# Two reorderings in a cross-attention kernel: where four probability casts stand while the pipeline fills, and the order of work as it drains

## The chip, the cores and the metric

The kernel runs on one core of a Trainium2 chip. The metric is the device time in microseconds (us), lower is better. A core has five engines, each with its own instruction stream that runs strictly in its written order: TensorE (PE, matrix products; its weight loads are shown as PEld), VectorE (DVE), ScalarE (ACT), GpSimd (POOL) and SyncE (SP), which here does nothing but issue DMA transfers. They meet through semaphores.

## What is computed

Cross-attention with four separate key sets per batch element. With 32 batch elements, 512 query rows, 640 channels, 20 heads of 32 channels, the inputs give 77 context rows, so that the first key set ("text", 77 keys) takes all of them and the other three are empty:

```python
q = _heads(hidden_states @ to_q_w)
h_txt = _sdpa(q, _heads(ehs_txt @ to_k_w), _heads(ehs_txt @ to_v_w))
...
out = _merge(h_txt) + ...
out = out @ to_out_w + to_out_b
out = (out + residual) / RESCALE
```

`_sdpa` is `softmax(q k^T / sqrt(32)) v` for each head, and the residual is the input itself.

## The kernel before

All products are made in pairs of numbers: every float32 operand is split into a high part (a cast to TensorE's rounded float32 type, made by ACT) and a low part (the operand less its high part, made by DVE or POOL), and a product is the sum of three matmuls: high by high, high by low, low by high.

**Opening (lines 294 to 383).** Keys and values of all batch elements are computed and put into DRAM scratch. Then comes the main pipeline.

**Groups and slots.** The 20 heads of a batch element are taken four at a time: five groups per element, `N` = 160 in all. Group `n` is batch element `b = n // 5` and chunk `j = n % 5`. `slot(n)` (line 661) writes out the instructions of all engines for one step of the pipeline, and the order in which it does so is the order of each engine's queue; no scheduler reorders anything. In slot `n`:

- PE: `scores(n, t)` for the four blocks `t` of 128 queries (three matmuls each; VectorE then reduces each block to the negated row maxima `nm`, line 462, and that reduction is queued right behind), `queries(n + 1)` in two parts of 6 and 9 matmuls, `values(n - 3)` (6 matmuls, line 546), and the output product of an earlier batch element, cut into pieces.
- ACT: `exps(n, t)`, four exponentials for each block (line 472); the high part of the next queries (`split_q`, line 103); the high parts of the probabilities of group n - 3 (`cast_p`, line 518, and the first line of `rest_p`, line 524); the copy `aw` that the sum of the attention's halves begins with (`sum_a`, line 557); the high part of the attention result of group n - 4 (`high_a`, line 566).
- DVE: the reductions; the low part of most of the probabilities (`rest_p`, line 525); the reciprocals of the row sums of group n - 1 (`sums`, line 482); low parts of the attention result (`low_a`, line 571) and of the queries (line 104); the transposition of the probabilities of group n - 1 into the single buffer `z` (`transpose_p`, line 494); the two additions of `sum_a` (line 559); the emptying of finished output banks (`finish`, line 618).
- POOL: `last_p` (line 532), the last low part of the probabilities; `normalize(n - 1)` (line 487), which multiplies the exponentials by the reciprocals and which the transposition waits for; low parts of the input `xt` (line 264); `add_bias` (line 582).
- SP: `load_p(n - 2)` (lines 510, 511) reads transposed probabilities from DRAM scratch `pd` into `raw`; then keys or values of the coming groups (`refill`), inputs `xs`, residual rows `xr`; the four transfers of `transpose_p` (line 501) that write `z` to `pd`; output rows.

So the probabilities of group n travel: normalized and transposed in slot n + 1, written to `pd`, loaded into `raw` in slot n + 2, cast and multiplied by the values in slot n + 3. Buffers that matter: `z` one, `raw` two, the parts `pp` one, the attention's bank pair `pa` one, banks for scores `sc` three, for queries `pq` one, and for the output `po` two. A third output bank can be begun only when VectorE has emptied the first.

**Two orders of the casts.** In a slot with output work (`has_out`; every slot from 7 on) `cast_p` opens the slot on ACT, ahead of the exponentials. The slots that have a group to take but no output product yet, 3, 4, 5 and 6, are marked `filling` (line 672); there the three functions stand behind the exponentials of the second block (line 711).

**The end.** The last slot, 159, returns after `values(156)` and the additions of `sum_a(156)`. `end()` (line 771) then writes out what is left: the last transposition, the attention's parts of group 156, the probabilities of 157, pieces 6 to 9 of the output of batch element 30, and then, with `take(157)`, `take(158)`, `take(159)` between them, the output of the last element. `piece(last - 1, 6)` closes the bank of rows block 2, first half, and then uses the other bank; `piece(last - 1, 7)` closes that one and begins block 3 in the bank that was closed first. `finish()` empties all banks that are closed.

Of the kernel before, what the change touches and what calls it, by code (L numbers as in the profile page):

```python
# [51 lines left out]
def kernel(  # L52
# [34 lines left out]
    N = B * NC_  # L87
# [403 lines left out]
    def transpose_p(n):  # L491

        pn = pnb[n % 2]
        nc.vector.transpose(  # L494
            z.rearrange("p b t j -> p t b j"),
            pn.rearrange("p (t h) k -> p t (h k)", t=NQ).rearrange("p t (b i) -> p t b i", i=Q),
        )
        pd = dram.tile([(NBLK + 2) * Q, S], F32, tag="pd", name="pd", bufs=6)
        rows = pd[: NBLK * Q].rearrange("(b i) q -> i b q", i=Q)
        for a in range(4):  # L500
            nc.sync.dma_start(
                rows[:, :, a * P : (a + 1) * P],
                z[a * Q : (a + 1) * Q].rearrange("p b t j -> p b (t j)"),
            )
        pds[n] = pd
# [8 lines left out]
    def cast_p(n):  # L514

        raw = raws[n]
        pp = late[0].tile([P, 5, S], FPR, tag="pp", name="pp", bufs=1)
        nc.scalar.copy(pp[:, 0:2, :], raw[:, 0:2, :])  # L518
        pps[n] = pp

    def rest_p(n):

        raw, pp = raws[n], pps[n]
        nc.scalar.copy(pp[:64, 4, :], raw[:64, 2, :])  # L524
        nc.vector.tensor_tensor(  # L525
            pp[:, 2:4, :], raw[:, 0:2, :], pp[:, 0:2, :].bitcast(F32), ALU.subtract
        )

    def last_p(n):

        raw, pp = raws.pop(n), pps[n]
        nc.gpsimd.tensor_tensor(  # L532
            pp[64:, 4, :], raw[:64, 2, :], pp[:64, 4, :].bitcast(F32), ALU.subtract
        )
# [26 lines left out]
    def high_a(n):  # L561
        if n >= N - NC_ + 1:
            at = xpool[0].tile([P, 2, S], FPR, tag="xt", name="at", bufs=7)
        else:
            at = late[0].tile([P, 2, S], FPR, tag="at", name="at", bufs=8)
        nc.scalar.copy(at[:, 0, :], pas[n][:, 0])
        ats[n] = at
# [93 lines left out]
    def slot(n, beside=()):  # L661
        b, j = divmod(n, NC_)
        ahead, more = n + 1 < N, b + 1 < B
        back, first = PIECES[j]
        bo_, has_out = b - back, b >= back
        xsplits = SPLIT_X.get(j, ((), ())) if more and n > LATE else ((), ())
        turns = TRANSPOSE_X.get(j, ((), (), ())) if more and b else ((), (), ())
        if b == 1 and j < 2:
            turns = (((), (), ()), ((0, 1), (2,), ()))[j]
        taken = takes.get(n)  # L670

        filling = taken is not None and not has_out
        if not filling:
            refill(b, j, 0)
        if taken is not None and not filling:
            cast_p(taken)
        if n - 1 in takes:
            high_a(takes[n - 1])
        s = scores(n, 0)
        if taken is not None and not filling:  # L680
            rest_p(taken)
        rs = sums(n - 1) if n else None
        if taken is not None and not filling:
            last_p(taken)
        if n:
            normalize(n - 1, rs)
        if n - 1 in takes:
            low_a(takes[n - 1])
        exps(n, 0, *s)
        if ahead:  # L690
            queries(n + 1, 0, 2)
        s = scores(n, 1)
        if n - LAG + 1 in pds and n > LATE:
            load_p(n - LAG + 1)
        if filling:
            refill(b, j, 0)
        if n == NC_:
            load_x(b + 1, (2, 3))
        for k in WO.get(n, ()):
            nc.sync.dma_start(wos[0][:, k].bitcast(F32), wo_dram[:, k].bitcast(F32))  # L700
        refill(b, j, 1)
        finish()
        if j == 4 and b and b + 2 < B:
            load_x(b + 2, (0, 1))
        if j in RESIDUAL and b >= RESIDUAL[j][0]:
            load_residual(b - RESIDUAL[j][0], RESIDUAL[j][1])
        if j in BIAS and b >= BIAS[j][0]:
            add_bias(b - BIAS[j][0], BIAS[j][1])
        exps(n, 1, *s)
        if filling:  # L710
            cast_p(taken)
            rest_p(taken)
            last_p(taken)
        for i in turns[0]:
            transpose_x(b + 1, i)
        if ahead:
            queries(n + 1, 2, NC_)
        s = scores(n, 2)
        if not ahead:
            exps(n, 2, *s)  # L720
            piece(bo_, first)
            s = scores(n, 3)
        if j == 3 and has_out:
            piece(bo_, first)
            finish()
        if n and has_out:
            transpose_p(n - 1)
        if ahead:
            split_q(n + 1)
            exps(n, 2, *s)  # L730
        if n and not has_out:
            transpose_p(n - 1)
        if j == 4 and b + 2 < B:
            load_x(b + 2, (0, 1) if not b else (2, 3))
        for c in xsplits[0]:
            split_x(b + 1, c)
        if not ahead:
            exps(n, 3, *s)
            normalize(n, sums(n))
            finish()  # L740
            piece(bo_, first + 1)
            values(taken)
            sum_a(taken)
            return
        if has_out:
            if j != 3:
                piece(bo_, first)
        else:
            s = scores(n, 3)
        if taken is not None:  # L750
            values(taken)
        if len(beside) > 0:
            context_values(LAST, beside[0], psv)
        if has_out:
            s = scores(n, 3)
        finish()
        for i in turns[1]:
            transpose_x(b + 1, i)
        if taken is not None:
            sum_a(taken)  # L760
        for c in xsplits[1]:
            split_x(b + 1, c)
        exps(n, 3, *s)
        if len(beside) > 1:
            context_values(LAST, beside[1], psv)
        if has_out:
            piece(bo_, first + 1)
        for i in turns[2]:
            transpose_x(b + 1, i)

    def end():


        last = B - 1
        load_p(N - 2)
        transpose_p(N - 1)
        high_a(N - 4)
        low_a(N - 4)
        cast_p(N - 3)
        rest_p(N - 3)  # L780
        last_p(N - 3)
        add_bias(last - 1, 3)
        piece(last - 1, 6)
        finish()
        piece(last - 1, 7)
        finish()
        load_p(N - 1)
        load_residual(last, 0)
        load_residual(last, 1)
        piece(last - 1, 8)  # L790
        take(N - 3)
        piece(last - 1, 9)
        cast_p(N - 2)
        rest_p(N - 2)
        last_p(N - 2)
        finish()
        spare = late[0].tile([P, 3, S], F32, tag="raw", name="xr", bufs=2)
        load_residual(last, 3, spare.rearrange("p k q -> p (k q)")[:, :C])
        load_residual(last, 2)

        def begin(i, j0, j1):
            t, h = divmod(i, 2)
            if j0 == 0:
                if i < 3:
                    pos[last, t, h] = ps.tile([P, S], F32, tag="sc", name="po", bufs=3)
                elif i == 3:
                    pos[last, t, h] = ps.tile([P, S], F32, tag="pq", name="po", bufs=1)
                elif i < 6:
                    output_bank(last, t, h)
                else:  # L810
                    if i == 6:
                        pas[N] = late[1].tile([P, 2, S], F32, tag="pa", name="po", bufs=1)
                    pos[last, t, h] = pas[N][:, i - 6]
            for j in range(j0, j1):
                project(last, t, h, j)

        begin(0, 0, 2)
        begin(1, 0, 2)
        take(N - 2)
        cast_p(N - 1)  # L820
        rest_p(N - 1)
        last_p(N - 1)
        for t in (0, 1, 3, 2):
            add_bias(last, t)
        begin(2, 0, 3)
        begin(0, 2, 4)
        begin(1, 2, 4)
        begin(2, 3, 4)
        begin(3, 0, 4)
        take(N - 1)  # L830
        begin(4, 0, 4)
        begin(5, 0, 4)

        def close(t):
            for h in range(2):
                project(last, t, h, 4)
                closed.append((last, t, h))
            finish()

        close(0)  # L840
        close(1)
        begin(6, 0, 4)
        close(2)
        begin(7, 0, 4)
        close(3)
# [65 lines left out]
```

## Time and profile before

Three timed runs lie between 1954.48 and 1955.75 us, with a median of 1954.53. The profiled execution took 1951.98 us; its span, from the first to the last instruction, is 1949.9 us. All positions below are us from the start of that span.

| stretch | us | PE busy | DVE busy | ACT busy | POOL busy | granted PE clock | DMA share |
|---|---|---|---|---|---|---|---|
| 0 to 301.87: keys, values, slots 0 to 2 | 301.87 | 290.97 | 134.82 | 93.80 | 53.67 | 0.99 | 0.84 |
| 301.87 to 344.74: slots 3 to 6 | 42.87 | 33.28 | 28.15 | 34.80 | 21.41 | 0.89 | 0.84 |
| 344.74 to 1895: slots 7 to 158 | 1550.26 | 1540.34 | 1249.10 | 1386.52 | 920.25 | 1.00 | 0.86 |
| 1895 to 1949.9: last slot and end | 54.90 | 40.70 | 25.57 | 18.79 | 19.84 | 0.94 | 0.48 |

A row gives the time in which each engine was at work within the stretch. "Granted PE clock" is the share of its full clock that the throttle let TensorE have. On PE's queue, slot 3 begins at 301.87 (first matmul of `scores`), slot 4 at 313.61, slot 5 at 324.56, slot 6 at 334.38 and slot 7 at 344.74.

In a timeline line the columns are start, duration, engine, line of the kernel, operation, what it writes and reads, how many; in brackets, how long the engine stood idle before it and who released it. In a line of the chain of waits the columns are start, duration and what the chain passed through.

### The profile page before, as it was taken

To read this page: it belongs to the slowest core of one execution; us is meant where nothing else is said; L and a number is where in the kernel's file an instruction comes from. 1 tells how busy PE (TensorE), PEld (TensorE's weight loads), DVE (VectorE), ACT (ScalarE), POOL (GpSimd) and SP (SyncE) were. 2 spreads that over 40 slices of the span, in tenths; PEclk is the share of its full clock that TensorE was granted. 3 is DMA by queue.
4 is the path that set the end of the run, shared out by engine and by line. 5 is a ranking of instruction groups with operands and counts; after the bars stand their busy time and mean duration, and the time that the engine had idled before them with its cause. 6 is when DMAs were issued, how large, how long until landed. Compare 5 with 4: busy or idle time off the path is not lost.

```text
span 1949.9 us, 36251 instructions
## 1 busy us (share of the span) xinstructions
PE 1905.3 (98%) x10332; PEld 1701.3 (87%) x10332; DVE 1437.6 (74%) x2334; ACT 1533.9 (79%) x6210; POOL 1015.2 (52%) x668
## 2 busy tenths in 40 slices
PE   9999998999999999999999999999999999999997
PEld 7787896889889989988889989988989999888896
DVE  4444345887888788787888878788888888877874
ACT  3232237898988898888888888898989989888982
POOL 1100055566556655555556555566655665556543
PEclk9999999999999999999999999999999999999999
DMA  9878878888888888988888888888889888888874
GB/s 185 190 188 232 201 198 215 222 226 230 228 225 230 227 229 228 239 232 218 227 238 233 229 225 228 236 232 224 228 232 237 227 229 225 225 224 232 230 201 144
DMA packets 560919, 431.28 MB, mean 221 GB/s; under 512 B 187024, under 2 KB 469072, under 8 KB 560720
## 3 DMA queue, kind: packets, MB, share of 16 engines
q1 hardware_dynamic: 556208, 414.46, 82.3%
q0 software_dynamic: 4416, 14.34, 2.2%
q8 instruction: 84, 1.38, 0.3%
q14 instruction: 115, 0.94, 0.2%
q10 hardware_dynamic: 96, 0.16, 0.0%
HBM read 247.17 MB, written 181.64 MB: 220 GB/s over the span
## 4 chain that ended last, share of the span: by engine, by line
PE 20%; ACT 19%; issue 17%; DMA 15%; DVE 13%; POOL 12%; SPq 2%; DVEq 0%; POOLq 0%; ACTq 0%
ACT pn L472 10%; POOL pn L487 8%; DMA raw<-pd 7%; DMA pd<-z 6%; PE pq L435 5%; PE po L589 5%; POOL pp L532 4%; DVE pp L525 3%; ACT xt L263 3%; ACT aw L557 3%; PE pk L191 2%; PE pv L191 2%; PE sc L454 2%; DVE nm L462 2%; DVE z L494 2%
## 5 line engine op out<-in xcount | busy, mean ns | idle before, releaser
L472 ACT ACTIVATE pn<-sc,nm 128x77 f32<-128x77 f32 x2560 | 802.5, 335 | 70.9 <-DVE nm L462 68.0
L589 PE MATMUL po<-wo_s,at 128*128 128x320 f32 x3840 | 624.3, 310 | 17.7 <-DVE xr L618 14.4
L435 PE MATMUL pq<-xt,wq_s 128*128 128x512 f32 x2400 | 605.4, 393 | 0.0
L589 PEld LDWEIGHTS po<-wo_s,at 128*128 128x128 f32 x3840 | 575.4, 188 | 27.8 <-DVE xr L618 24.6
L532 POOL TENSOR_TENSOR pp<-raw,pp 64x512 fp32r<-64x512 f32 x160 | 211.8, 1324 | 643.6 <-ACT pp L524 413.4
L472 ACT ACTIVATION_READ_ACCUMULATOR pn<-sc,nm 128x1 f32 x2560 | 545.1, 213 | 0.0
L435 PEld LDWEIGHTS pq<-xt,wq_s 128*128 128x128 f32 x2400 | 436.8, 188 | 75.1
L454 PE MATMUL sc<-kb,qt 128*128 128x308 f32 x1920 | 377.5, 305 | 1.3 <-ACT pn L472 0.5
L487 POOL TENSOR_TENSOR pn<-pn,rs 128x1232 f32<-128x1232 f32 x160 | 364.4, 2277 | 24.7 <-DVE rs L482 12.6
L494 DVE STREAM_TRANSPOSE z<-pn 128x1280 f32<-128x1280 f32 x160 | 241.8, 1511 | 168.8 <-POOL pn L487 158.4
L454 PEld LDWEIGHTS sc<-kb,qt 128*128 128x128 f32 x1920 | 325.7, 189 | 45.0 <-ACT pn L472 1.6
L462 DVE TENSOR_REDUCE nm<-sc 128x4 f32<-128x308 f32 x640 | 295.1, 462 | 46.4 <-PE sc L454 44.1
L546 PE MATMUL pa<-pp,vb 128*128 128x512 f32 x960 | 256.0, 401 | 10.5 <-ACT pp L518 4.8
L525 DVE TENSOR_TENSOR pp<-raw,pp 128x1024 fp32r<-128x1024 f32 x160 | 195.6, 1222 | 88.2 <-ACT pp L518 78.9
L559 DVE TENSOR_TENSOR pa<-pa,aw 64x512 f32<-64x512 f32 x320 | 222.6, 696 | 34.7 <-ACT aw L557 25.2
L557 ACT COPY aw<-pa 64x1024 f32<-64x1024 f32 x160 | 162.0, 1012 | 79.6 <-PE pa L546 77.4
L264 POOL TENSOR_TENSOR xt<-xs,xt 128x512 fp32r<-128x512 f32 x160 | 204.3, 1296 | 37.1 <-ACT xt L263 35.3
L546 PEld LDWEIGHTS pa<-pp,vb 128*128 128x128 f32 x960 | 175.3, 190 | 43.8 <-ACT pp L518 5.8
L582 POOL TENSOR_TENSOR xr<-xr,bias 128x640 f32<-128x640 f32 x128 | 201.5, 1575 | 0.2
L518 ACT CAST pp<-raw 128x1024 fp32r<-128x1024 f32 x160 | 168.9, 1055 | 33.0 <-DMA raw<-pd 33.0
L191 PE MATMUL pk<-ct,wk_s 128*128 128x512 f32 (+1 forms) x600 | 137.9, 388 | 9.1 <-ACT ct L103 6.4
L191 PEld LDWEIGHTS pk<-ct,wk_s 128*128 128x128 f32 x600 | 114.2, 191 | 31.1 <-ACT ct L103 7.3
(43 smaller groups left out, 1358.0 us busy)
## 6 DMA issues: line engine op xcount, KB each, us to landing
pd<-z SPq DMA_DIRECT2D x640, 160.0 KB, 3.8
raw<-pd SPq DMA_DIRECT2D x160, 512.0 KB, 4.0
xs<-in_x_dram SPq DMA_DIRECT2D x128, 320.0 KB, 6.2
xr<-in_x_dram SPq DMA_DIRECT2D x128, 320.0 KB, 4.1
out_dram<-xr SPq DMA_DIRECT2D x127, 320.0 KB, 4.1
raw<-pd SPq DMA_DIRECT2D x160, 128.0 KB, 4.2
v_dram<-vs SPq DMA_DIRECT2D x80, 192.0 KB, 3.9
k_dram<-ks POOLq DMA_DIRECT2D x20, 512.0 KB, 3.7
```

What stands on the lines that cost most here:

```text
L191: nc.tensor.matmul(held[j][:, :gn], w[:, k, a, :], cts[g, k][:, c, :gn], start=(k == 0 and n == 0), stop=(k == NK - 1 and n == 2),)
L435: nc.tensor.matmul(pqs[n], wq_s[:, k, a, j * P : (j + 1) * P], xts[b, k][:, c, :], start=(k == 0 and m == 0), stop=(k == NC_ - 1 and m == 2),)
L454: nc.tensor.matmul(sc[:, :KCOLS], qt[:, a, t * P : (t + 1) * P], kb[:, j - GROUPS[g][0], c], start=(m == 0), stop=(m == 2),)
L462: nc.vector.tensor_reduce(nm, sc[:, :KCOLS].rearrange("p (h k) -> p h k", k=NKEY), AX.X, ALU.max, negate=True)
L472: nc.scalar.activation(pnb[n % 2][:, at, :NKEY], sc[:, i * NKEY : (i + 1) * NKEY], AF.Exp, bias=nm[:, i : i + 1], accum_out=sms[n][:, at : ...
L487: nc.gpsimd.tensor_tensor(pf, pf, rs.unsqueeze(2).to_broadcast([P, NQ * HPC, NKEY]), ALU.mult)
L494: nc.vector.transpose(z.rearrange("p b t j -> p t b j"), pn.rearrange("p (t h) k -> p t (h k)", t=NQ).rearrange("p t (b i) -> p t b i", i=Q),)
L525: nc.vector.tensor_tensor(pp[:, 2:4, :], raw[:, 0:2, :], pp[:, 0:2, :].bitcast(F32), ALU.subtract)
L532: nc.gpsimd.tensor_tensor(pp[64:, 4, :], raw[:64, 2, :], pp[:64, 4, :].bitcast(F32), ALU.subtract)
L546: nc.tensor.matmul(pas[n][:, p, :], vb[:, p, t, :], pp[:, c, :], start=(c == p), stop=(t == 1),)
L559: nc.vector.tensor_tensor(pa[64 * p : 64 * p + 64, 0], pa[:64, p], aw[:, p], ALU.add)
L589: nc.tensor.matmul(pos[b, t, h][:, :HALF], ats[b * NC_ + j][:, a, t * P : (t + 1) * P], wos[0][:, j, c, h * HALF : (h + 1) * HALF], start= ...
```

## The change

In `slot`, the condition `not filling` is taken off `cast_p`, `rest_p` and `last_p`, and the separate place for filling slots is removed: slots 3 to 6 take the order that all later slots have. `refill` keeps its two places. In `end`, piece 6 and the emptying of its closed bank come first; the casts of group 157 on ACT keep their order after `high_a`; `low_a` stands behind `cast_p`, which are on different engines; and the last transposition, with its four transfers, comes behind the second `finish`.

```diff
@@ slot
         filling = taken is not None and not has_out
         if not filling:
             refill(b, j, 0)
-        if taken is not None and not filling:
+        if taken is not None:
             cast_p(taken)
         if n - 1 in takes:
             high_a(takes[n - 1])
         s = scores(n, 0)
-        if taken is not None and not filling:
+        if taken is not None:
             rest_p(taken)
         rs = sums(n - 1) if n else None
-        if taken is not None and not filling:
+        if taken is not None:
             last_p(taken)
...
         exps(n, 1, *s)
-        if filling:
-            cast_p(taken)
-            rest_p(taken)
-            last_p(taken)
         for i in turns[0]:
             transpose_x(b + 1, i)
@@ end
         load_p(N - 2)
-        transpose_p(N - 1)
+        piece(last - 1, 6)
+        finish()
         high_a(N - 4)
+        cast_p(N - 3)
         low_a(N - 4)
-        cast_p(N - 3)
         rest_p(N - 3)
         last_p(N - 3)
         add_bias(last - 1, 3)
-        piece(last - 1, 6)
-        finish()
         piece(last - 1, 7)
         finish()
+        transpose_p(N - 1)
         load_p(N - 1)
```

## The prediction

> **What bounds it now.** I read the busy shares first, then the waits of TensorE, then busy time by stretch, then the timelines of the two places that the change touches.
>
> ```profile
> PE 1905.3 (98%) x10332; PEld 1701.3 (87%) x10332; DVE 1437.6 (74%) x2334; ACT 1533.9 (79%) x6210; POOL 1015.2 (52%) x668
> ```
>
> TensorE bounds the middle: between 345 and 1895 it waits 8.1 us in all. A lead won ahead of that stretch is carried through it; the end is a chain of its own. The end first, a timeline from 1904:
>
> ```profile
> 1904.40 1.43 DVE L559 TENSOR_TENSOR pa<-pa,aw 64x512 f32<-64x512 f32 x2 [0.57 <-ACT aw L557]
> 1905.86 0.59 ACT L566 CAST at<-pa 128x512 fp32r<-128x512 f32 x1 [1.49 <-DVE pa L559]
> 1906.35 1.05 ACT L518 CAST pp<-raw 128x1024 fp32r<-128x1024 f32 x1
> ...
> 1908.64 1.51 DVE L494 STREAM_TRANSPOSE z<-pn 128x1280 f32<-128x1280 f32 x1 [2.81 <-DMA pd<-z]
> ...
> 1910.07 0.65 DVE L571 TENSOR_TENSOR at<-pa,at 128x512 fp32r<-128x512 f32 x1
> ...
> 1910.65 1.34 DVE L525 TENSOR_TENSOR pp<-raw,pp 128x1024 fp32r<-128x1024 f32 x1
> 1911.91 0.87 DVE L618 TENSOR_TENSOR xr<-po,xr 128x320 f32<-128x320 f32 x2
> 1912.44 4.42 PE L589 MATMUL po<-wo_s,at 128*128 128x320 f32 x18 [6.10 <-DVE xr L618]
> ```
>
> ```profile
> 1906.30:1912.40 6.10, 0.04 (x1) 0.00 (x0) 3.76 (x5) 1.61 (x3) 2.79 (x2) 0.72 0.76 215
> 1912.40:1916.90 4.50, 4.46 (x19) 4.45 (x20) 0.39 (x1) 0.00 (x0) 0.00 (x0) 0.62 0.69 211
> ```
>
> The second view gives busy time of PE, PEld, DVE, ACT, POOL, then granted clock and DMA. PE stands from 1906.34 to 1912.44 because both output banks are closed and not emptied. The emptying (line 618) is queued on DVE behind the last transposition, which waited 2.81 us for `z` to be written out, then behind `low_a` and `rest_p`. When PE resumes, its clock is 0.62: 18 matmuls take 4.42 us, 0.246 each, where the next 24 take 3.67, 0.153 each.
>
> Now the fill, slot 4:
>
> ```profile
> 319.90 1.05 ACT L518 CAST pp<-raw 128x1024 fp32r<-128x1024 f32 x1
> ...
> 321.00 0.49 PE L546 MATMUL pa<-pp,vb 128*128 128x512 f32 x1 [1.44 <-ACT pp L518]
> 322.26 2.50 PE L546 MATMUL pa<-pp,vb 128*128 128x512 f32 x5 [0.77 <-DVE pp L525]
> ```
>
> ```profile
> 326.03 3.35 DMA pd<-z
> ...
> 329.94 6.93 DMA raw<-pd
> ...
> 337.86 4.37 DMA pd<-z
> ```
>
> PE waits for the casts before each `values`. But ACT is busy 34.80 of the fill's 42.87 us, which no order changes, and the chain of waits (second fence) leaves the engines for the relay of `z` through DRAM.
>
> **The end, worked out.** Nothing is added or removed; PE's order stays. New DVE order: the first emptying follows the additions at once, 1905.85 to 1906.30 (0.44 each, half of 0.87). PE resumes 0.09 after an emptying (1912.35 to 1912.44 now), so at 1906.40, and does six matmuls of block 3 and the nine that begin piece 8 (15 x 0.153 = 2.3): 1908.7. The next bank needs the second emptying. DVE does `low_a` (needs `high_a`, 1906.45) to 1907.15, `rest_p` after the cast's end, 1907.42 to 1908.68, the emptying to 1909.12; PE begins the bank at 1909.21, three matmuls to 1909.7. `last_p` stays at 1908.04 to 1909.30, so the parts of 157 are ready: `values(157)` starts near 1909.70 instead of 1916.55 to 1916.70. That is 6.9 us: 6.0 of standing and 18 x 0.093 = 1.7 of the slow clock, less 0.5 for the new wait on the second bank and 0.3 by which `values` overlaps the matmuls ahead of it now.
>
> Whether the rest moves along depends on what is now late. The last transposition goes from 1908.64 to 1909.15, its end from 1910.15 to 1910.66. On SP it is moved past one output transfer and stays ahead of the last `load_p` and two residual loads. Its four transfers start near 1910.7 instead of 1910.18; `load_p(159)` follows at 1916.02 + 0.5 and lands 3.9 later, 1920.4 to 1921.0 with its second part. `cast_p(159)`, 1928.65 now, would be wanted at 1921.7: slack 0.7. `values(159)` has 0.6 more, since PE, not the parts (POOL ends at 1932.11), holds it until 1932.72. `raw` of 158 is issued at 1908.65 and lands 4.0 later, 1912.7, wanted at 1914.3. Residual rows land by 1923, wanted by the bias at 1925.2. So the whole tail shifts: **-6.9 us**. If the relay of 159 came 2 us later than worked, 1.3 to 0.7 of it would be lost; if PE regained its clock only by 1913, another 1. Bounds -5 to -7.4 (no second-bank wait).
>
> **The fill, worked out.** ACT steps from slot 4: cast 0.93, its second line 0.52, four blocks of exponentials 4 x 1.21, `high_a` 0.48, query split 0.5, `aw` 1.03: 8.3 us a slot whatever the order, against slots of 9.8 to 11.7 now. In the new order the loop that closes is: exponentials of block 3 end, cast 1.05, `rest_p` 1.14, reciprocal 0.2, and on POOL `last_p` to 1.3 (1.75 where it meets DVE) and `normalize` 2.27, transposition 1.45, reduction 0.45, exponentials 1.21.
>
> Slot 3: the third block's exponentials of slot 2 end at 306.58 as now; cast to 307.54, `rest_p` to 308.81, reciprocal 309.0, `normalize` 309.65 to 312.1, transposition to 313.6, its block 3 exponentials 314.9 to 316.1 (now 315.72 to 316.93): 0.8 won. `raw` of 1, issued at 310.19 with 3.8 to 4.2 to landing, is there by 314.9. Slot 4: cast 316.13, `rest_p` 317.2 to 318.34, reciprocal 318.55, `normalize` from 319.65 or 320.1, transposition of 3 from 321.95 or 322.4 to 323.4 or 323.85, now 324.61: 0.75 to 1.2 won. ACT alone would go on winning: slot 6's block 3 could begin 1.7 to 2.6 earlier. But then the relay decides. SP is free in slot 4 (last issue at 321.25), so the transfers of 3 move by that 0.75 to 1.2, and with them, each waiting for the one before, the load of `raw` 3 (6.93 to landing, behind input rows), the transfers of 4 and, behind eight value loads on SP (3.86), those of 5, whose landing near 353.65 lets slot 7's transposition, of group 6, begin (353.87 now). The split of group 8's queries is queued behind that on DVE, and PE waits for it even now (0.29 at 356.01). So PE, up to 2.7 ahead in slot 7, hands all but the relay's lead back at slot 8: **-0.9 us**.
>
> What covers the moved casts: in slot 6 `raw` of 3 lands at about 335.5 (336.4 now less 0.9), ACT arrives at about 334.9, so the cast waits 0.6 with the exponentials queued behind it; covered, since the relay is later still. Without any lead in the relay the fill gives 0; without the limit at slot 8, -2.7. Bounds 0 to -2.7; I take the relay's own.
>
> [...] The fill's rows have PE at clock 0.95 in 320 to 322, 0.50 in 322 to 324 and 0.70 in 324 to 326, after waits of 1.44 and 0.77 only. [...]
>
> **Sum.** -6.9 - 0.9 = -7.8 on the profiled 1951.98: 1944.2. The median is 2.55 above it, so 1954.53 - 7.8 = **1946.7**.
>
> **Rivals.**
> 1. The fill gives nothing, the end all: the relay's lead is lost in the full DMA of slots 5 and 6 (1.22 in the rows from 336 to 340). 1954.53 - 6.9 = 1947.6. For: transfers there already take 4.5 to 6.9 us. Against: the issues themselves come earlier.
> 2. The fill's lead is kept: the transfers of 5 land early enough not to hold slot 7's transposition. 1954.53 - 6.9 - 2.7 = 1944.9. Against: the 0.29 wait at 356.01.
> 3. A new wait at the end: the last relay lands some 5 us late and `cast_p(159)` waits. 5.0 less 1.3 slack loses 3.7: 1950.4. For: the transposition that feeds it does start later, behind everything. Against: half of DMA is idle there (share 0.48).
> 4. Slower: the casts at the opening stand on ACT for late `raw` with every exponential behind them. Place: slots 4 to 7; price: the waits themselves, once they exceed the 1.5 us a slot (9.8 less 8.3) that ACT can make up. Should each load take 6.9 as that of 3 does (2.9 above 4.0) and push the next relay by 0.6, that is 3.5 a slot, 14 in four, less the slack of 6: 8 net, 1954.53 - 6.9 + 8 = 1955.6. It decides from 7 us of net loss. Against: loads of 0, 1, 2 and 4 took 3.7 to 5.4, and all but that of 3 are there before ACT comes.
>
> **Numbers.** Forecast 0.60 (own range 1945.5 to 1948.0), rival 1 0.16, 2 0.08, 3 0.08, 4 0.08. Changes within 0.2%, 3.9 us, can't be told from none: faster means below 1950.6. The forecast and rivals 1 and 2 lie there (0.84) with 0.02 of rival 3: faster 0.86; the rest of rival 3 and 0.01 of rival 4 within, 0.07; slower 0.07. The range runs from rival 2 with the best end (1944.9 less 0.5, less the spread of 1.3 that the three runs show) to rival 3's edge: 1943.3 to 1950.2.
>
> **What would show it.** Right: PE idle 0.1 to 0.6 instead of 6.1 near 1900; clock 1.00 in the matmuls behind it; the last transposition idle under 0.2 for its buffer; `values(157)` some 7 us earlier before the last instruction. In the fill: `values` with no wait for line 518 or 525, the wait now at the fourth `scores`; a cast that waits for `raw` in slot 6 alone; slot 8 beginning near 354.4 on PE. Wrong: a wait of `cast_p(159)` above 1.3 us, slot 7 beginning after 345, or the middle stretch longer than 1550 us by more than the lead.

## The result and the profile after

The changed kernel is faster by half a percent: ratio 0.9948, 95% interval 0.9931 to 0.9965, medians 1942.84 against 1954.48 us over seven runs each. A second comparison, further down, gives 0.9954 (0.9942 to 0.9966). On the 1954.53 us that the forecast was made from, the first ratio is 1944.4 and the second 1945.5; the forecast was 1946.7, with 1945.5 to 1948.0 as its own narrower range. The median itself lies 0.5 below the whole range's low end of 1943.3.

The profiled execution took 1942.15 us with a span of 1940.2, 9.7 less than before. First the end, a timeline of the changed kernel from 1901 (start, duration, engine, line, what it writes and reads, number, idle time ahead of it and who ended that):

```profile
1901.04 4.84 PE L589 MATMUL po<-wo_s,at 128*128 128x320 f32 x30 [0.19 <-DVE xr L618]
...
1902.89 0.47 DVE L618 TENSOR_TENSOR xr<-po,xr 128x320 f32<-128x320 f32 x1
...
1903.63 0.69 DVE L571 TENSOR_TENSOR at<-pa,at 128x512 fp32r<-128x512 f32 x1 [0.27 <-ACT at L566]
...
1904.58 1.23 DVE L525 TENSOR_TENSOR pp<-raw,pp 128x1024 fp32r<-128x1024 f32 x1 [0.26 <-ACT pp L518]
...
1905.72 0.48 DVE L618 TENSOR_TENSOR xr<-po,xr 128x320 f32<-128x320 f32 x1
...
1906.12 1.50 DVE L494 STREAM_TRANSPOSE z<-pn 128x1280 f32<-128x1280 f32 x1
...
1906.26 0.70 PE L589 MATMUL po<-wo_s,at 128*128 128x320 f32 x3 [0.38 <-DVE xr L618]
...
1906.81 1.55 PE L546 MATMUL pa<-pp,vb 128*128 128x512 f32 x6
```

The first emptying (line 618 at 1902.89) stands right behind the attention's additions, so the 15 matmuls that a wait of 6.10 us followed before now run on into the next 15. TensorE waits 0.38 for the second bank, and the last transposition finds its buffer free. The windows beside it (busy PE, PEld, DVE, ACT, POOL, granted clock, DMA):

```profile
1901.00:1905.90 4.90, 4.84 (x30) 4.40 (x30) 3.79 (x6) 2.57 (x4) 2.70 (x2) 1.00 0.82 208
1905.90:1912.00 6.10, 5.61 (x33) 5.08 (x33) 3.54 (x5) 2.06 (x3) 2.61 (x2) 1.00 0.87 248
```

The granted clock is 1.00; in the two windows of before, the wait and the matmuls behind it, it was 0.72 and 0.62. Then the fill, TensorE's timeline of the changed kernel in slots 4, 7 and 8:

```profile
319.82 0.69 PE L454 MATMUL sc<-kb,qt 128*128 128x308 f32 x3 [1.58 <-ACT pn L472]
320.35 1.56 PE L546 MATMUL pa<-pp,vb 128*128 128x512 f32 x6
...
341.96 0.59 PE L454 MATMUL sc<-kb,qt 128*128 128x308 f32 x3
...
354.83 0.41 PE L454 MATMUL sc<-kb,qt 128*128 128x308 f32 x1 [2.12 <-DVE qt L104]
355.08 2.48 PE L435 MATMUL pq<-xt,wq_s 128*128 128x512 f32 x6
```

`values` (line 546) runs without a wait; the wait is now ahead of the fourth `scores`, as forecast. Slot 7 begins at 341.96, 2.78 earlier. But the first block of scores in slot 8, begun at 352.27, waits 2.12 ahead of its third matmul, the one that needs the low part of the queries (line 104), and the six query matmuls behind it take 2.48 instead of 1.55: the granted clock is 0.85 from 354 to 356 and 0.50 from 356 to 358.

To follow a lead along the kernel I take the start of each group's normalization on GpSimd (line 487), in one profile and in the first profile of before, both counted from group 0's. "Tail" is the time from group 159's normalization to the last instruction. All in us; positive is earlier. Group n is normalized in slot n + 1.

| profile | lead at group 6 | 9 | 11 | 159 | tail |
|---|---|---|---|---|---|
| before (first) | 0 | 0 | 0 | 0 | 46.33 |
| before, again | 0.61 | 0.18 | -1.16 | 0.84 | 46.27 |
| changed (first) | 2.85 | 1.18 | 0.54 | 3.06 | 39.49 |
| changed, again | 2.75 | 0.79 | 0.74 | 1.44 | 39.81 |
| fill alone | 2.66 | 0.54 | -0.05 | 1.89 | 48.33 |
| fill alone, again | 3.55 | 1.13 | 1.20 | 1.69 | 48.43 |
| end alone | -0.01 | -0.01 | 0.55 | 2.32 | 39.42 |
| emptying first | 0.00 | 0.03 | 0.45 | 1.54 | 43.07 |
| transposition last | 0.61 | -0.16 | -0.73 | 1.54 | 44.64 |
| query split first | 2.99 | 0.66 | 0.91 | 1.67 | 39.78 |
| two buffers z | 2.23 | 0.10 | -0.27 | -1.33 | 40.83 |
| matmuls in the wait | 3.28 | 2.00 | 0.84 | 1.58 | 39.80 |

The first pair of profiles splits into 6.84 at the tail, 3.06 up to it, and 0.20 lost ahead of group 0's normalization, where neither part has changed anything: 9.7. The 3.06 is not all the fill's: only 0.54 of it is there at group 11, and 2.5 come in the middle, whose code is the same. The experiments had to say whether that is an effect or chance.

### The profile page after: what moved, and what is told of

Its sections match the earlier page's. It is cut to its first block, busy times and chain, and to the rows that moved or that the text cites. A ratio compares the mean times of both kernels' runs of the same rounds, so it can differ in the third digit from the quotient of the medians.

```text
span 1940.2 us, 36252 instructions
## 1 busy us (share of the span) xinstructions
PE 1906.9 (98%) x10332; PEld 1701.8 (88%) x10332; DVE 1439.4 (74%) x2334; ACT 1534.2 (79%) x6210; POOL 1015.0 (52%) x668
## 4 chain that ended last, share of the span: by engine, by line
PE 22%; issue 19%; ACT 18%; DMA 14%; DVE 13%; POOL 12%; SPq 3%; DVEq 0%; POOLq 0%; ACTq 0%
ACT pn L472 9%; POOL pn L487 8%; DMA raw<-pd 6%; PE pq L435 6%; PE po L589 6%; DMA pd<-z 5%; POOL pp L532 3%; DVE pp L525 3%; PE sc L454 3%; ACT aw L557 3%; ACT xt L263 3%; PE pa L546 3%; PE pk L191 2%; PE pv L191 2%; DVE nm L462 2%
```

## The experiments

Theory A is the forecast's, sharpened: the end gives 6.8, the fill's lead is handed back soon after slot 7, and the middle's 2.5 is chance. Theory B: the fill shifts the middle lastingly.

**Fill alone** (the end as before):

```diff
@@ end
-        piece(last - 1, 6)
-        finish()
+        transpose_p(N - 1)
...
+        piece(last - 1, 6)
+        finish()
         piece(last - 1, 7)
         finish()
-        transpose_p(N - 1)
         load_p(N - 1)
```

> The fill's part alone, the end as before. Theory A (the fill's lead is mostly given back at slots 8 and 9, where TensorE waits 2.1 us for the transposition ahead of the query split and then runs at half clock; the rest of what the middle won is chance): slot 7 begins some 2.8 us earlier on TensorE than before, slot 10 at most 0.7 earlier; time 0.3 to 1 us less, ratio 0.9990 to 1.0005. Theory B (the fill's shift sets the middle stretch lastingly, as the first look suggests): 2.5 to 3.5 us less, ratio 0.9982 to 0.9987, and the waits of TensorE for line 618 in the middle stay near 4.5 us. Theory C (it costs): ratio above 1.001.

Ratio 0.9995 (0.9984 to 1.0005): the interval takes in no change at all, and of theory B's band only the upper part. The lead is 2.66 at group 6 and -0.05 at group 11, as A has it.

**End alone** (`slot` as before):

```diff
@@ slot
-        if taken is not None:
+        if taken is not None and not filling:
             cast_p(taken)
... (the same for rest_p and last_p)
         exps(n, 1, *s)
+        if filling:
+            cast_p(taken)
+            rest_p(taken)
+            last_p(taken)
```

> The end's part alone, the fill as before. Theory A: from the additions of the last slot's attention sum to the last instruction 6.8 us less than before; ratio 0.9960 to 0.9968. Theory B: the same 6.8 at the end, with the middle as before; ratio near 0.9965, and clearly above the whole change's 0.9948. Rival for the end (a late load of the last probabilities takes part of the gain): 3 to 5 us, ratio 0.9975 to 0.9985.

Ratio 0.9963 (0.9949 to 0.9977), 7.2 us; the tail is 39.42 against 46.33, 6.9 less. The rival with a late load falls. But its profile also gains 2.32 up to group 159, with a fill and a middle that were not touched. In this series of runs the savings of the two parts add up to a ratio of 0.9958; the whole has 0.9954 (below).

**Before, again**, no edit:

> The kernel before, unchanged, with a second profile. Theory A: the waits of TensorE for line 618 between 345 and 1895 differ from the first profile's 8.1 us by 2 us or more, and the start of each group's normalization wanders by 1 to 3 us against the first profile without any edit; ratio 0.999 to 1.001. Theory B: 7.5 to 8.7 us again and a wander below 0.7 us.

Ratio 0.9994 (0.9984 to 1.0004). TensorE's waits in the middle, one line each from the waits of the first profile of before, of this one and of the changed kernel (engine, line and releaser; total us, times, longest):

```profile
PE po L589 <- DVE xr L618: 8.1, 14, 1.0
```

```profile
PE po L589 <- DVE xr L618: 6.6, 7, 1.9
```

```profile
PE po L589 <- DVE xr L618: 4.5, 9, 1.0
```

The total differs by 1.5 between two executions of the same code, a little under the 2 expected; the lead wanders from 0.61 to -1.16 and back to 0.84, within the 1 to 3 expected. Over the five profiles without the fill's edit the lead at group 159 runs from 0 to 2.32. The first profile of before is simply the slowest of them in the middle.

These waits are what makes the middle long or short. From group 11's normalization to group 159's the first profile of before takes 1500.60 us and this one 1498.61, and TensorE waits 7.1 and 4.8 of them, all for line 618. The two profiles of the changed kernel take 1498.09 and 1499.91, with 4.5 and 5.9; the two of the fill alone 1498.67 and 1500.12, with 5.0 and 5.7. So two executions of the same code differ there by 1.4 to 2.0 us, and most of it is output banks emptied late. Why they are late in one and not in the next stays open.

**Changed, again**, no edit:

> The changed kernel again, with a second profile. Theory A: the lead at slot 10 is again 0.2 to 0.7 us and at the end's beginning anywhere from 0 to 4; ratio 0.9955 to 0.9968. Theory B: the middle wins 2.5 us again; ratio 0.9945 to 0.9952.

Ratio 0.9954 (0.9942 to 0.9966), just below the 0.9955 that theory A allowed. Its lead is 0.74 at group 11 and 1.44 at group 159: the middle won 0.7 this time, not 2.5. Theory B's lasting 2.5 does not hold.

**Query split first.** What takes the fill's lead? In slot 7 the split of group 8's queries is queued behind the transposition of group 6. Here it goes ahead:

```diff
-        if n and has_out:
+        if n and has_out and n != 7:
             transpose_p(n - 1)
         if ahead:
             split_q(n + 1)
             exps(n, 2, *s)
-        if n and not has_out:
+        if n and (not has_out or n == 7):
             transpose_p(n - 1)
```

> The changed kernel with one order turned in slot 7: the split of the next queries stands ahead of the transposition of group 6 on VectorE, as it does in slots without output work. Theory A (the fill's lead of 2.8 us is handed back in slot 8, where TensorE waits 2.1 us for the query split behind the held transposition and then pays 1.6 us at half clock): the wait at the first scores of slot 8 falls from 2.1 to below 0.4 us, the clock stays at 1.00, and the lead at slot 10, counted from slot 2's opening, is 2.0 to 3.0 us instead of 0.0 to 0.7. Rival (the lead is lost to DMA or ScalarE in slots 8 to 10 anyway): the wait goes, another takes its place, the lead at slot 10 stays below 1.0. Time: ratio 0.994 to 0.9955.

Ratio 0.9965 (0.9951 to 0.9978). The wait for line 104 goes, and this is what stands in slot 8 instead, in TensorE's timeline of this kernel:

```profile
357.25 0.56 PE L589 MATMUL po<-wo_s,at 128*128 128x320 f32 x2 [0.70 <-ACT at L566]
358.73 0.98 PE L589 MATMUL po<-wo_s,at 128*128 128x320 f32 x4 [0.92 <-DVE at L571]
359.51 2.76 PE L546 MATMUL pa<-pp,vb 128*128 128x512 f32 x6
```

and ahead of it on ScalarE, from the same kernel:

```profile
355.66 1.05 ACT L518 CAST pp<-raw 128x1024 fp32r<-128x1024 f32 x1 [0.38 <-DMA raw<-pd]
```

TensorE now waits for the attention's parts of group 4, whose high part is queued behind the opening cast of slot 8, and that waits 0.38 for its load. `values` then takes 2.76 (1.55 otherwise), with the granted clock at 0.82 from 358 to 360 and 0.50 from 360 to 362. The lead is 0.66 at group 9 and 0.91 at group 11, where theory A expected 2.0 to 3.0: the rival is right, another wait takes the place of the one removed.

**Two buffers for the transposed probabilities:**

```diff
-    z = main.tile([P, NBLK, NQ, Q], F32, name="z")
+    zs = [main.tile([P, NBLK, NQ, Q], F32, name=f"z{n}") for n in range(2)]
...
-        pn = pnb[n % 2]
+        pn, z = pnb[n % 2], zs[n % 2]
```

> The changed kernel with two buffers for the transposed probabilities instead of one. Theory A (what holds slot 7's transposition at 352.69 is the landing of the transfers of group 5 out of the single buffer, 1.5 us after its normalization): it starts within 0.1 us of the normalization's end, TensorE's wait at slot 8's first scores falls from 2.1 to about 0.6 us, the lead at slot 10 is 1.0 to 2.5. In the end the last two transpositions no longer wait for a landing, which changes nothing there, since they are off the path. Rival (it waits for GpSimd's bias addition, which ends at the same moment): no change, the transposition still starts near 1.5 us after the normalization.

The timelines of GpSimd and VectorE in slot 7, first of the changed kernel:

```profile
348.90 2.28 POOL L487 TENSOR_TENSOR pn<-pn,rs 128x1232 f32<-128x1232 f32 x1
```

```profile
352.69 1.51 DVE L494 STREAM_TRANSPOSE z<-pn 128x1280 f32<-128x1280 f32 x1 [2.82 <-POOL xr L582]
```

and then of this one, which runs some 5 us later from the opening on:

```profile
354.69 2.28 POOL L487 TENSOR_TENSOR pn<-pn,rs 128x1232 f32<-128x1232 f32 x1
```

```profile
357.01 1.51 DVE L494 STREAM_TRANSPOSE z<-pn 128x1280 f32<-128x1280 f32 x1 [1.33 <-POOL pn L487]
```

The transposition starts 0.04 after its normalization ends (356.97), where in the changed kernel 1.51 lay between the two (351.18 to 352.69). So the single buffer was what held it, as the prediction read it, and not the bias addition (line 582) that the bracket names, which here has only just begun. The lead is not kept for all that: 0.10 at group 9, where 1.0 to 2.5 was expected, and -0.27 at group 11, with waits of 0.48, 0.63, 0.51 and 0.93 in slots 7 and 8 in place of the 2.12. The opening cast of slot 8 now waits 1.71 for its load. Ratio 0.9969 (0.9956 to 0.9983).

**Matmuls in the wait:** 14 products of the high parts, overwritten by the real ones, ahead of slot 8's first scores.

```diff
@@ scores
+        if (n, t) == (8, 0):
+            for _ in range(14):
+                nc.tensor.matmul(sc[:, :KCOLS], qt[:, 0, t * P : (t + 1) * P],
+                                 kb[:, j - GROUPS[g][0], 0], start=True, stop=True)
```

> The changed kernel with 14 more matmuls of 308 columns ahead of slot 8's first scores, into the same bank, overwritten by the real ones: TensorE is at work during the wait, which itself stays. Theory A (the wait of 2.1 us costs a second time through the clock): granted clock 1.00 instead of 0.50 to 0.85 after the wait, queries of slot 8 in 1.55 and 2.2 us instead of 2.48 and 2.56, lead at slot 10 higher by 1.2 to 1.7 us. Rival (the clock does not matter, since the later engines are late anyway): same clock effect but the lead at slot 10 unchanged within 0.4.

Windows of the changed kernel, then of this one:

```profile
354.00:356.00 2.00, 1.17 (x4) 1.02 (x5) 1.93 (x5) 0.80 (x5) 1.25 (x1) 0.85 0.92 320
356.00:358.00 2.00, 2.00 (x7) 1.62 (x6) 1.49 (x3) 2.00 (x7) 0.00 (x0) 0.50 0.78 213
358.00:360.00 2.00, 2.00 (x9) 1.69 (x8) 1.82 (x4) 1.83 (x10) 1.33 (x2) 0.80 1.12 329
```

```profile
354.00:356.00 2.00, 1.89 (x10) 1.52 (x10) 1.93 (x5) 1.42 (x9) 0.67 (x1) 1.00 0.96 281
356.00:358.00 2.00, 2.00 (x12) 1.71 (x11) 1.49 (x3) 2.00 (x5) 0.02 (x1) 1.00 0.93 306
358.00:360.00 2.00, 2.00 (x14) 1.87 (x13) 2.00 (x7) 1.84 (x13) 1.92 (x2) 1.00 1.00 273
```

The clock stays at 1.00, the queries take 1.55 and 2.23, and the lead at group 9 is 2.00 instead of 1.18 and 0.79: 0.8 to 1.2 more, where theory A expected 1.2 to 1.7. At group 11 it is 0.84, against 0.54 and 0.74: theory A's clock effect is there, and the rival is right about what it is worth two slots later. The ratio, 0.9946 (0.9928 to 0.9965), can't be told from the changed kernel's.

What levels all of them is slot 11. Its opening cast waits for its load in all twelve profiles, with the fill's edit and without, 1.32 to 2.33 us. Four of them, each from ScalarE's timeline: before, changed, fill alone, matmuls in the wait (whose added lines move line 518 to 527):

```profile
389.30 1.05 ACT L518 CAST pp<-raw 128x1024 fp32r<-128x1024 f32 x1 [1.89 <-DMA raw<-pd]
```

```profile
388.95 1.05 ACT L518 CAST pp<-raw 128x1024 fp32r<-128x1024 f32 x1 [2.04 <-DMA raw<-pd]
```

```profile
391.33 1.05 ACT L518 CAST pp<-raw 128x1024 fp32r<-128x1024 f32 x1 [2.00 <-DMA raw<-pd]
```

```profile
388.46 1.06 ACT L527 CAST pp<-raw 128x1024 fp32r<-128x1024 f32 x1 [2.33 <-DMA raw<-pd]
```

Counted from group 0's normalization, which in them starts 0.20, 1.99 and 0.01 later than in the first profile of before, the casts of the three start 0.55 earlier, 0.04 later and 0.85 earlier than there; their leads at group 11 are 0.54, -0.05 and 0.84. In all twelve, the probabilities that it waits for, group 8's, take 7.3 to 8.5 us from the first issue of their writing to the landing and another 5.6 to 6.8 to be loaded. In "matmuls in the wait" a lead of 2.01 at their transposition is 1.16 when they are written and 0.59 when they are loaded. So at slot 11 the lead is the relay's, not the engines'.

**The two halves of the end.** In both, the fill is as before. Emptying first, with the transposition right behind the first `finish` (against the end of the changed kernel):

```diff
         piece(last - 1, 6)
         finish()
+        transpose_p(N - 1)
         high_a(N - 4)
...
         finish()
-        transpose_p(N - 1)
         load_p(N - 1)
```

> The end's first half alone, the fill as before: the first output bank is emptied ahead of the attention's parts, but the last transposition follows at once, ahead of the parts, and not behind the second emptying. Theory A: TensorE resumes at once and then waits for the second bank, whose emptying stands behind the transposition (held until the landing of the transfers before it, 2.8 us) and the parts: a wait of 3.0 to 3.5 us at that bank instead of 6.1 at the first; of the 6.8 us some 3.5 to 4.5 remain. Rival (the transposition's place does not matter once the first bank is empty): 6.5 or more remain.

Transposition last, with the emptying where it was before (against the end of before):

```diff
         load_p(N - 2)
-        transpose_p(N - 1)
         high_a(N - 4)
...
         finish()
+        transpose_p(N - 1)
         load_p(N - 1)
```

> The end's second half alone, the fill as before: the last transposition goes behind the emptying of both banks, but both banks are still emptied only after the attention's parts. Theory A (the 6.1 us are the sum of two queues on VectorE, about 3.4 us of the transposition with its wait and about 2.7 of the parts): the first wait of TensorE falls from 6.1 to 2.6 to 3.0 us, none at the second bank, and 3.3 to 5 of the 6.8 us remain. Together with the empty-first half, which kept 3.3 from its tail, the halves add up to about the whole. Rival (the transposition alone is the cause): the wait falls below 1 us and 6 or more remain.

TensorE's timelines, of the first and then of the second:

```profile
1911.06 0.71 PE L589 MATMUL po<-wo_s,at 128*128 128x320 f32 x3 [3.77 <-DVE xr L618]
```

```profile
1908.09 4.46 PE L589 MATMUL po<-wo_s,at 128*128 128x320 f32 x18 [2.74 <-DVE xr L618]
...
1925.21 5.04 PE L589 MATMUL po<-wo_s,at 128*128 128x320 f32 x22 [0.16 <-DVE at L571]
```

The waits are 3.77 at the second bank (3.0 to 3.5 expected, so a little more) and 2.74 at the first (2.6 to 3.0 expected). From group 159's normalization to `values(157)` it is 13.13 us before, 9.48 and 9.82 with the halves, 6.10 with both: 3.65 and 3.31 come to 6.96 of the whole 7.03. The tails keep only 3.26 and 1.69, so both halves miss what was expected of them (3.5 to 4.5 and 3.3 to 5). In both, later matmuls ran slower than before. Behind the 3.77, `values(157)` and the 24 matmuls after it took 1.94 and 4.87, where before they took 1.55 and 3.67. In "transposition last" the 22 matmuls late in the tail took 5.04, at a granted clock of 0.62 from 1925 to 1929, where before they took 3.50. Ratios 0.9990 (0.9977 to 1.0003) and 0.9982 (0.9969 to 0.9994).

**Fill alone, again:**

> The fill's part alone once more, with a second profile. Theory A (the lead won in the fill, 2.7 us on GpSimd at slot 7, is handed back by slot 11 to the relay through DRAM): relative to slot 0 the lead is again 2.5 to 3.0 at group 6's normalization and -0.3 to 0.9 at group 11's; the tail behind group 159's normalization is 46.3 us, or up to 2 more where the clock is late; ratio 0.9985 to 1.0005. Theory B (2.5 us or more are kept): lead at group 11 above 1.5, ratio below 0.9985.

Ratio 1.0003 (0.9990 to 1.0015). The lead is 3.55 at group 6, above the band, and 1.20 at group 11, 0.3 above it too; below the 1.5 of theory B. Both profiles of the fill alone have a tail of 48.3 to 48.4, 2 longer than before's with the same waits: the 18 and the 22 matmuls there take 4.9 and 5.0 instead of 4.42 and 3.50, with the granted clock at 0.59 from 1913 to 1918 in the second of them and at 0.65 and 0.50 from 1930 to 1934 in the first. In these two profiles the longer tail takes back all of the 1.89 and 1.69 won up to group 159. That the fill causes it is not shown; the same 22 matmuls took 5.04 in "transposition last" too, whose fill is that of before.

## Why the prediction was right

*The bound.* Right: an end with its own chain, a middle that carries what it is given. At group 159 the four profiles with the fill's edit that are otherwise the recorded kernels have an average lead of 2.02, the five without it 1.25: 0.77 between them, where it was about 0.8 at group 11. From slot 7's first scores to group 159's normalization the first profiles take 1558.83 us before (1903.57 less 344.74) and 1558.75 after (1900.71 less 341.96). That they agree so closely is luck: 2.3 of the lead was lost by group 11, and 2.5 came back by chance.

*The end, -6.9.* Right in place, mechanism and size: 7.03 to `values(157)`, 6.84 at the tail, 7.2 by the ratio of the end alone. The steps: the run of matmuls without a gap (forecast 0.1 to 0.6 of idle, measured 0.19 and 0.38), clock 1.00, the new wait on the second bank (0.5 forecast). `cast_p(159)` did not wait for its load. Two things went otherwise without changing the sum. The 14 matmuls behind `values(158)` took 3.99, with the granted clock at 0.50 from 1916 to 1918 and 0.82 in the 2 us on either side; they only filled the time in which TensorE waited 1.47 for the attention's cast before. And SP's last residual loads took 5.63 to issue, unnoticed, since the bias addition comes later.

*The fill, -0.9.* The mechanism was right: PE 2.8 ahead at slot 7, then held to the lead of the relay through DRAM. Each step up to slot 7 was met within 0.6 us (block 3's exponentials of slot 3 at 315.28 for 314.9, the transposition of group 3 at 322.39 for 321.95 to 322.4, a cast waiting 0.67 for its load in slot 6; another 0.24 in slot 7 was not forecast). Slot 8 did not begin near 354.4 on PE but at 352.27, since only its third matmul had to wait; that one came at 354.83, 1.18 earlier than before. The step that was off is the one that settled the rest at slot 8, "hands all but the relay's lead back at slot 8": what was left, 1.18, 0.79, 0.54 and 1.13 at group 9, was half or nothing in two of the four by slot 11, whose load is late in any order. At group 11 those four profiles average 0.61, the five without the edit -0.18: about 0.8, with single profiles scattered by up to 1.0 around these. By time the fill alone is 0.9995 and 1.0003, no difference that can be measured. Rival 1, in which the end is all, is as close to this as the forecast. The first result of 1944.4 lies nearest to rival 2 (1944.9), in which the fill's lead is kept; that is chance, since the lead of 2.2 to 3.6 at group 6 is down to -0.3 to 1.2 at group 11 in all seven profiles with the fill's edit.

*The clock.* The forecast's sum has no term for the granted clock in the fill. In slots 4 and 5 it stayed at 1.00 after waits of 1.58. Behind the waits of 1.98 in slot 3, 2.41 in slot 6 and 2.12 in slot 8 it fell to 0.50 (312 to 314), 0.56 (340 to 342) and 0.50 (356 to 358), in slot 8 with TensorE at the front. There it cost 0.93, 0.38 and 0.33 on the next three runs of matmuls (2.48, 0.97 and 2.56 for 1.55, 0.59 and 2.23). That was then swallowed by slot 11.

*Small slips.* TensorE's waits between 345 and 1895 come to 8.4 us, of which 8.1 are for line 618. By its own terms the low end of the range is 1944.9 less 0.5 less 1.3, 1943.1 and not 1943.3, and rival 3 stands at 1950.4, not at 1950.2. Nothing here hangs on either.

*What was missing.* The first profile shows 9.7 against 7.8. The difference of 1.9 is the middle's 2.5 less 0.6 elsewhere, and the 2.5 are chance: from group 11 on, two executions of the same kernel differ by 1.4 to 2.0 us in three pairs of profiles, and TensorE's waits for output banks emptied late differ with them (7.1 and 4.8, 4.5 and 5.9, 5.0 and 5.7). A single pair of profiles can't price an edit to better than that; the leads at fixed points and the ratios can.

No version measured beats the changed kernel by more than its interval.

## What to carry to other kernels

Look at what stands ahead of a small instruction that frees the bounding engine's next buffer: moving two emptyings of 0.45 us past work and waits that ended 6 us later, on an engine with time to spare, won all of the gain that can be measured here, and the two halves of that queue added up (3.65 and 3.31 of 7.03). Before moving work earlier, follow the data it needs through every buffer and transfer; here, where a relay through DRAM set the pace, a lead of 2.85 us at group 6 was 0.54 at group 11. And price a wait on TensorE twice, once for the wait and once for the clock that can fall behind it (to 0.50 behind the 2.12 in slot 8, while it stayed at 1.00 behind the 1.58 in slot 4), but only where TensorE, not another engine, sets the pace there.

## What the runs showed of the hardware

In the tails the granted clock does not follow from the waits alone. The same four waits (0.67, 0.76, 0.17, 1.47, within 0.01) are followed by 22 matmuls in 3.50 us in both profiles of before, and in 5.03 or 5.04 in three others (both of the fill alone and "transposition last"). In the first profile of the changed kernel the clock falls some 4 us earlier, to 0.50 from 1916 to 1918, on the 14 matmuls behind `values(158)`, and the 22 take 3.49. Windows around the 22, first of before, where they begin at 1929.53, then of the fill alone, where they begin at 1930.09:

```profile
1928.00:1930.00 2.00, 1.03 (x5) 0.77 (x6) 1.09 (x3) 1.83 (x3) 0.00 (x0) 1.00 0.41 137
1930.00:1932.00 2.00, 2.00 (x16) 2.00 (x15) 0.96 (x1) 0.21 (x1) 1.65 (x1) 1.00 0.00 0
```

```profile
1928.00:1930.00 2.00, 0.56 (x2) 0.30 (x2) 1.35 (x2) 1.28 (x2) 0.00 (x0) 1.00 0.58 168
1930.00:1932.00 2.00, 1.91 (x9) 1.91 (x10) 1.26 (x2) 0.77 (x2) 1.10 (x1) 0.65 0.00 0
1932.00:1934.00 2.00, 2.00 (x9) 2.00 (x9) 0.00 (x0) 0.00 (x0) 1.92 (x2) 0.50 0.00 0
```

The waits just ahead of them are 1.47 and 0.17 in the first, 1.47 and 0.16 in the second; the clock behind them is 1.00 in the first and 0.65, then 0.50 in the second. So some 1.5 us of this chain hang on it (5.03 less 3.50). What decides between the two is not shown.
